# Rows of exponentials for graph attention: a trip through DRAM in place of transposes

## Chip, cores, metric

The kernel runs on one core of a Trainium2 chip. The metric is the device time of one execution in microseconds (us). Nearly all executions agree within 0.3%. Engines: TensorE does matmuls (PE in the profile; PEld are its weight loads), VectorE elementwise work (DVE), ScalarE activations and evictions (ACT), GpSimd (POOL) a little, SyncE issues DMAs (SP, its queue SPq).

## The reference, cut to what matters

64 graphs of 256 nodes with 256 features pass two layers: a graph attention layer (two attention steps, then a feed-forward) and a transformer-like layer with relations. Only the graph attention steps matter here, twice per graph:

```python
e = Wh1 + swapaxes(Wh2, 1, 2)          # [N, 1] + [1, N]
e = leaky_relu(e, 0.2)
att = softmax(where(adj > 0, e, NEG), axis=1)
h = matmul(att, Wh)
```

Because exp is monotonic, exp(leaky_relu(a + b)) is the larger of exp(a)exp(b) and exp(0.2a)exp(0.2b). So the kernel needs, on every partition, a row of exp(a) over all nodes and a row of exp(0.2a), and one number per partition for b.

## The kernel before

Graphs go in pairs; three pairs are in flight. A generator per pair yields after each step, and a small ordering rule hands the steps out: `yield us, later, stage` says how long the step takes on TensorE and how long to wait before the next step of the same pair is due. Steps of other pairs fill the wait. This only sets the order in which the program is written; the compiler's scheduler then orders each engine's queue. The argument below takes each engine to work through its queue in that order; experiment 5 shows ScalarE held so for 25.83 us by one operation.

```python
def addends(y, at, layer, pair, b):
    ...
    nc.scalar.activation(rise[:, 0], e1, AF.Exp, bias=shift[:, 0:1])
    nc.scalar.activation(rise[:, 1], e1, AF.Exp, bias=shift[:, 0:1], scale=ALPHA)
    nc.scalar.activation(ratio, e2, AF.Exp, scale=ALPHA - 1.0)
    return rise, ratio                       # rise: [128, 2, 2], four columns

def gat_weights(y, at, rise, ratio, adjT, empty, b):
    p = bank()
    for n in range(4):                       # L199: repeated column -> row on all partitions
        col = rise[:, n // 2, n % 2:n % 2 + 1]
        nc.tensor.transpose(p[:, n * P:(n + 1) * P], col.to_broadcast([P, P]), ident)
    up = work.tile([P, N], F32, name="up", bufs=2)
    nc.scalar.activation(up, p[:, :N], AF.Copy)
    ...                                      # e from p, ratio, up, adjT (VectorE)
    ...                                      # y scaled by 1/sums (ScalarE, L212)
```

A pair's graph attention is: product xT x w12 (L227), evictions, `addends`, `gat_weights`, product with e (L241), evictions, `addends`, `gat_weights`, product with e (L253), layer norm. Four transposes for each of 2 graphs and 2 layers make 16 per pair. The main filler is the feed-forward: L289 transposes x, ScalarE evicts yT (L290), L308 and L319 are its two matmul groups, L311 its activation.

## Time and profile before

| | before |
|---|---|
| time | 3452.26 us, median of 3 (3450.34 to 3454.68) |
| TensorE busy | 3344.4 us, 97% |
| VectorE, ScalarE busy | 55%, 40% |
| period (two pairs) | 213.4 us |
| first store of results | 225.7 us after the start |

A row of the profile's groups reads: line, engine, operation, tiles, shapes, count, then busy time in all, mean of one in ns, and idle time of the engine in front of it with what ended it. A row of waits reads: who waited for whom, us in total, times, longest. The lines themselves stand in the prediction.

### The profile page before, as it was taken

Reading aid. Unit: us, or ns where it says so; the run is one execution under the profiler, and the core shown is the slowest. Engines: PE = TensorE matmul, PEld = TensorE weight load, DVE = VectorE, ACT = ScalarE, POOL = GpSimd, SP = SyncE. Lnnn points to the kernel's source line nnn. Section 1 sums busy time; section 2 is a strip of 40 time slices with the busy share of each in tenths; the row PEclk is TensorE's granted clock in tenths of the full one; section 3 lists DMA queues with packets and bytes.
Section 4 is the critical chain, followed back from the end, with each engine's and each line's share of the span. In section 5 each row is a group of like instructions: output and inputs, shape, how many; then the busy total and the mean of one; then the engine's idle time right before and its main releaser. Section 6 shows DMA issues by size and latency. Waiting matters only on the chain.

```text
span 3449.2 us, 47284 instructions
## 1 busy us (share of the span) xinstructions
PE 3344.4 (97%) x18698; PEld 2150.5 (62%) x18698; DVE 1904.6 (55%) x4825; ACT 1371.0 (40%) x2586; POOL 481.5 (14%) x646
## 2 busy tenths in 40 slices
PE   7999999999999999999999999999999999999998
PEld 5566665666656566565665666656666566565655
DVE  5655645556456564555645555465554655546455
ACT  4343343433434334343444434444253442534332
POOL 0201111011110111111111111111111111111110
PEclk9999999999999999999999999999999999999999
DMA  5000010000100001000000100001000010000000
GB/s 166 7 25 19 13 37 7 25 19 13 37 7 25 25 7 37 7 28 23 20 25 7 41 10 25 19 7 43 7 25 19 7 43 7 25 19 1 13 1 14
DMA packets 66868, 78.22 MB, mean 23 GB/s; under 512 B 3280, under 2 KB 57680, under 8 KB 66640
## 3 DMA queue, kind: packets, MB, share of 16 engines
q1 hardware_dynamic: 66640, 75.13, 7.0%
q8 instruction: 150, 2.46, 0.3%
q14 instruction: 78, 0.64, 0.1%
HBM read 58.34 MB, written 16.78 MB: 22 GB/s over the span
## 4 chain that ended last, share of the span: by engine, by line
PE 87%; ACT 9%; DVE 2%; DMA 1%; issue 0%; SPq 0%; POOL 0%; POOLq 0%; DVEq 0%
PE ps L319 26%; PE ps L308 23%; PE ps L342 7%; PE ps L335 6%; PE ps L388 6%; PE ps L360 4%; PE ps L381 4%; PE ps L253 3%; PE ps L405 3%; ACT L189 2%; ACT yT L290 2%; PE ps L241 2%; PE ps L227 2%; PE ps L289 1%; ACT ff L311 1%; DVE e L206 1%
## 5 line engine op out<-in xcount | busy, mean ns | idle before, releaser
L276 POOL TENSOR_TENSOR rstd<-rstd,mhalf 128x2 f32<-128x2 f32 x256 | 206.1, 805 | 2729.3 <-DVE rstd L275 2713.4
L308 PE MATMUL ps<-yT,w_L_gnn_W 128*128 128x512 f32 x1024 | 482.7, 602 | 14.2 <-ACT yT L290 12.5
L308 PE MATMUL ps<-yT,w_L_gnn_w_ff 128*128 128x512 f32 x1024 | 482.5, 602 | 14.1 <-ACT yT L290 12.5
L319 PE MATMUL ps<-w_L_gnn_w_ff,ff 128*128 128x256 f32 x2048 | 450.2, 379 | 0.0
L319 PE MATMUL ps<-w_L_gnn_W,ff 128*128 128x256 f32 x2048 | 449.9, 379 | 0.0
L319 PEld LDWEIGHTS ps<-w_L_gnn_W,ff 128*128 128x128 f32 x2048 | 389.1, 190 | 66.6 <-issue 15.3
L319 PEld LDWEIGHTS ps<-w_L_gnn_w_ff,ff 128*128 128x128 f32 x2048 | 389.0, 190 | 66.0 <-issue 14.8
L374 DVE TENSOR_TENSOR m<-a,adjT 128x512 f32<-128x512 f32 x512 | 327.0, 688 | 175.6 <-ACT a L365 134.9
L266 DVE TENSOR_TENSOR x<-ps,x 128x512 f32<-128x512 f32 x256 | 176.1, 688 | 444.3 <-PE ps L319 330.7
L311 ACT ACTIVATE ff<-ps,c_L_gnn_b_ff 128x512 f32<-128x512 f32 x256 | 176.0, 687 | 448.2 <-PE ps L308 448.2
L365 ACT ACTIVATE a<-ps 128x512 f32<-128x512 f32 x512 | 264.4, 602 | 216.3 <-PE ps L360 216.1
L337 DVE TENSOR_TENSOR v<-ps,b_L_gnn_bv 128x512 f32<-128x512 f32 x128 | 88.1, 689 | 400.5 <-PE ps L335 400.5
L308 PEld LDWEIGHTS ps<-yT,w_L_gnn_W 128*128 128x128 f32 x1024 | 183.0, 190 | 199.2 <-issue 174.1
L308 PEld LDWEIGHTS ps<-yT,w_L_gnn_w_ff 128*128 128x128 f32 x1024 | 183.1, 190 | 198.9 <-issue 174.2
L290 ACT ACTIVATE yT<-ps 128x512 f32<-128x512 f32 x192 | 110.2, 592 | 479.8 <-PE ps L289 479.8
L311 ACT ACTIVATE ff<-ps,c_L_gnn_b 128x512 f32<-128x512 f32 x256 | 175.9, 687 | 292.8 <-PE ps L308 292.4
L335 PE MATMUL ps<-wv,yT 128*128 128x512 f32 x512 | 235.4, 592 | 0.0
L229 ACT ACTIVATE xw<-ps 128x260 f32<-128x260 f32 x128 | 45.7, 379 | 456.0 <-PE ps L227 456.0
L394 DVE RECIPROCAL s<-ps 128x256 f32<-128x256 f32 x128 | 224.0, 1750 | 0.0
L273 DVE BATCH_NORM_STATS2 st<-x 128x6 f32<-128x256 f32 x512 | 192.7, 418 | 8.6
L206 DVE SCALAR_TENSOR_TENSOR e<-ps,ratio,up 128x256 f32<-128x256 f32 x256 | 115.7, 475 | 141.2 <-ACT up L201 141.2
L335 PEld LDWEIGHTS ps<-wv,yT 128*128 128x128 f32 x512 | 97.3, 190 | 122.5 <-issue 122.2
(81 smaller groups left out, 4290.1 us busy)
## 6 DMA issues: line engine op xcount, KB each, us to landing
xT<-in_xT SPq DMA_DIRECT2D x32, 512.0 KB, 4.6
adjT<-in_adjT SPq DMA_DIRECT2D x32, 512.0 KB, 3.9
x<-in_x SPq DMA_DIRECT2D x32, 512.0 KB, 4.2
out<-x SPq DMA_DIRECT2D x32, 512.0 KB, 3.2
w_L_gnn_w_ff<-in_L_gnn_w_ff SPq DMA_DIRECT2D x2, 1024.0 KB, 11.3
w_L_gnn_W<-in_L_gnn_W SPq DMA_DIRECT2D x2, 1024.0 KB, 7.0
wv<-in_L_gnn_Wv SPq DMA_DIRECT2D x2, 256.0 KB, 7.1
w_L_gnn_W1T<-in_L_gnn_W1T SPq DMA_DIRECT2D x1, 256.0 KB, 6.1
```

The costliest lines, as they stand in the source:

```text
L273: nc.vector.bn_stats(st[:, j, :], r[:, 2 * b + j, :])
L276: nc.gpsimd.tensor_tensor(rstd, rstd, mhalf[:, :2], ALU.pow)
L290: nc.scalar.activation(yT[:, :, b * N:(b + 1) * N], pt.rearrange("p (c n) -> p c n", c=KC), AF.Copy)
L308: nc.tensor.matmul(p1, lhsT=w1[:, c, m * P:(m + 1) * P], rhs=yT[:, c, :], start=c == 0, stop=c == KC - 1)
L311: nc.scalar.activation(h, p1, func, bias=b1[:, m:m + 1])
L319: nc.tensor.matmul(p2[:, j * D:(j + 1) * D], lhsT=f[m][:, k * P:(k + 1) * P], rhs=w2[:, m, :], start=m == 0, stop=m == NF - 1)
L335: nc.tensor.matmul(ps, lhsT=yT[:, c, at:at + P], rhs=wv[:, c].rearrange("p r m -> p (r m)"), start=c == 0, stop=c == KC - 1)
L342: nc.tensor.matmul(ps, lhsT=w[:, d, c * P:(c + 1) * P], rhs=yT[:, d, :], start=d == 0, stop=d == KC - 1)
L365: nc.scalar.activation(a, ps[o], AF.Exp)
L374: nc.vector.tensor_tensor(m, a, adj, ALU.mult)
L388: nc.tensor.matmul(po[o * DH:(o + 1) * DH, :N], lhsT=v[:, jc, at:at + DH], rhs=ms[o][:, jc * N:(jc + 1) * N], start=r == 0 and jc == 0, st ...
L394: nc.vector.reciprocal(s, po[:, N:])
```

## The change

The row is fetched by DMA, so that TensorE gives up the transposes: `rise` is scattered to a row in DRAM, and that row is read back onto all 128 partitions. To hide the latency, the steps are ordered with longer delays; the load of the next pair and the store of the results move to later places.

```diff
+    scratch = ctx.enter_context(tc.tile_pool(name="scratch", bufs=4, space=bass.MemoryType.DRAM))
 ...
-    p = bank()
-    for n in range(4):
-        col = rise[:, n // 2, n % 2:n % 2 + 1]
-        nc.tensor.transpose(p[:, n * P:(n + 1) * P], col.to_broadcast([P, P]), ident)
-    up = work.tile([P, N], F32, name="up", bufs=2)
-    nc.scalar.activation(up, p[:, :N], AF.Copy)
+    row = scratch.tile([1, 4 * P], F32, name="row")
+    nc.sync.dma_start(row.rearrange("o (n p) -> p (o n)", p=P), rise.rearrange("p n j -> p (n j)"))
+    rows = work.tile([P, 2, N], F32, name="rows", bufs=4)
+    nc.sync.dma_start(rows.rearrange("p n i -> p (n i)"), row.to_broadcast([P, 4 * P]))
 ...
-            yield 1.75, b * 1.6, None            # after the first layer's product
+            yield 1.75, b * 6.5, None
 ...
-            yield 0.5, b * 3.4, None             # after each graph's weights
+        yield 0.0, 3.4, None
 ...                                              # the same in the second layer
-        nc.sync.dma_start(out[...], x)
-        yield 3.44, 0.0, None
+        yield 3.44, 5.0, None
+        nc.sync.dma_start(out[...], x)
```

In the new kernel the first product with e is L239, the second still L253.

More of the change, by code (lines that the diff above doesn't have):

```diff
@@ L191, in addends, with gat_weights @@
         nc.scalar.activation(ratio, e2, AF.Exp, scale=ALPHA - 1.0)
-        return rise, ratio
-    def gat_weights(y, at, rise, ratio, adjT, empty, b):
-        p = bank()
-        for n in range(4):
-            col = rise[:, n // 2, n % 2:n % 2 + 1]
-            nc.tensor.transpose(p[:, n * P:(n + 1) * P], col.to_broadcast([P, P]), ident)
-        up = work.tile([P, N], F32, name="up", bufs=2)
-        nc.scalar.activation(up, p[:, :N], AF.Copy)
+        row = scratch.tile([1, 4 * P], F32, name="row")
+        nc.sync.dma_start(row.rearrange("o (n p) -> p (o n)", p=P), rise.rearrange("p n j -> p (n j)"))
+        rows = work.tile([P, 2, N], F32, name="rows", bufs=4)
+        nc.sync.dma_start(rows.rearrange("p n i -> p (n i)"), row.to_broadcast([P, 4 * P]))
+        return rows, ratio
+    def gat_weights(y, at, rows, ratio, adjT, empty, b):
         e = work.tile([P, 2, N], F32, name="e", bufs=4)
@@ L205, in gat_weights @@
             k = 2 * b + j
-            nc.vector.scalar_tensor_tensor(e[:, j], p[:, N:], ratio[:, j:j + 1], up, op0=ALU.mult, op1=ALU.max)
+            nc.vector.scalar_tensor_tensor(e[:, j], rows[:, 1], ratio[:, j:j + 1], rows[:, 0], op0=ALU.mult, op1=ALU.max)
             nc.vector.scalar_tensor_tensor(e[:, j], adjT[:, k], empty[:, k:k + 1], e[:, j],
@@ L230, in gat_layers @@
             a.append(addends(y, D + 2, 0, pair, b))
-            yield 1.75, b * 1.6, None
-        if pair + 1 < NPAIR:
-            loaded[pair + 1] = load(pair + 1)
+            yield 1.75, b * 6.5, None
         for b in range(2):
             e.append(gat_weights(y, D + 2, *a.pop(0), adjT, empty, b))
-            yield 0.5, b * 3.4, None
+        yield 0.0, 3.4, None
         for b in range(2):
@@ L244, in gat_layers @@
             a.append(addends(z, D, 1, pair, b))
-            yield 1.75, 0.4 + b * 0.6, None
+            yield 1.75, b * 6.5, None
         for b in range(2):
             e.append(gat_weights(z, D, *a.pop(0), adjT, empty, b))
-            yield 0.5, b * 3.4, None
+        if pair + 1 < NPAIR:
+            loaded[pair + 1] = load(pair + 1)
+        yield 0.0, 3.4, None
         for b in range(2):
```

## The prediction

> **What bounds the kernel now.** I read the page first: busy shares, then the chain that ended last. The chain gives 87% of the span to TensorE, so the question is only what happens to TensorE's queue.
>
> ```profile
> span 3449.2 us, 47284 instructions
> PE 3344.4 (97%) x18698; PEld 2150.5 (62%) x18698; DVE 1904.6 (55%) x4825; ACT 1371.0 (40%) x2586; POOL 481.5 (14%) x646
> PE 87%; ACT 9%; DVE 2%; DMA 1%; issue 0%; SPq 0%; POOL 0%; POOLq 0%; DVEq 0%
> q1 hardware_dynamic: 66640, 75.13, 7.0%
> ```
>
> TensorE is idle for 3449 - 3344 = 105 us in all. VectorE and ScalarE have half their time to spare, the DMA engines nine tenths. The list of waits says where the 105 us lie; the start takes most of the rest.
>
> ```profile
> PE ps L199 <- ACT rise L189: 29.6, 46, 0.9
> PE ps L308 <- ACT yT L290: 25.0, 34, 0.7
> PE ps L253 <- ACT xw L212: 21.0, 16, 3.0
> ```
>
> L199 are the transposes to be removed; they also head the list of waits, because they follow two exps that follow an eviction. L253 is the second layer's product, L308 the feed-forward behind its own transposes (L289). To see what L199 really holds of the queue I read TensorE's timeline in the middle of the run (start, length, instructions, idle before). The pattern repeats every 213.4 us with two pairs of graphs in it.
>
> ```profile
> 1505.31 1.04 PE L289 MATMUL ps<-ident,x 128*128 128x128 f32 x8
> 1506.18 0.60 PE L199 MATMUL ps<-ident,rise 128*128 128x128 f32 x4
> 1507.31 0.65 PE L199 MATMUL ps<-ident,rise 128*128 128x128 f32 x4 [0.52 <-ACT rise L189]
> 1508.07 3.70 PE L308 MATMUL ps<-yT,w_L_gnn_W 128*128 128x512 f32 x8
> ...
> 1518.52 0.60 PE L199 MATMUL ps<-ident,rise 128*128 128x128 f32 x4
> 1520.04 0.65 PE L199 MATMUL ps<-ident,rise 128*128 128x128 f32 x4 [0.92 <-ACT rise L189]
> 1520.53 3.60 PE L308 MATMUL ps<-yT,w_L_gnn_W 128*128 128x512 f32 x8
> 1525.32 1.99 PE L253 MATMUL ps<-xw,e 128*128 128x256 f32 x8 [1.20 <-ACT xw L212]
> ...
> 1562.85 1.04 PE L199 MATMUL ps<-ident,rise 128*128 128x128 f32 x8
> 1563.72 3.60 PE L308 MATMUL ps<-yT,w_L_gnn_w_ff 128*128 128x512 f32 x8
> ...
> 1587.85 1.04 PE L289 MATMUL ps<-ident,x 128*128 128x128 f32 x8
> 1589.63 3.70 PE L308 MATMUL ps<-yT,w_L_gnn_w_ff 128*128 128x512 f32 x8 [0.74 <-ACT yT L290]
> ```
>
> Read from start to start, eight transposes with no wait take 1563.72 - 1562.85 = 0.87 us. A group with a wait takes 1508.07 - 1506.18 = 1.89 or 1520.53 - 1518.52 = 2.01. One period has groups of 1.88, 2.01, 1.88 and 0.87: 6.65 us.
>
> **What the Trainium skill says.** "DMA: Bandwidth & Descriptors", section "Anatomy of one DMA", puts a fixed cost near 2 us on a DMA, mostly the receipt of the last write, heaviest where the target is HBM. The trace fits: the 512 KB output store lands a median 3.2 us after issue (2.9 at best). The same page, "Two DMAs through the same engine are not ordered", says that a DMA reading what another wrote must wait for the first one's semaphore before it is issued: so two landings in series, which no DMA of this trace shows. Its "Rules for kernel authors" say that a non-contiguous last dimension becomes one descriptor per element: the first new DMA scatters 512 elements of 4 bytes. The nearest thing here, the 2 KB load of a1 in small runs, kept SyncE 0.65 us to issue against 0.37 for a 512 KB load. "TensorE: Matmul & The Clock Gate", "Part 4: PE-mode transpose", has some 275 ns for a transpose; the trace has 273 ns for one alone but 0.87/8 = 109 ns in a row, and I use the latter.
>
> **Removed.** Per layer and pair eight transposes on TensorE, two evictions of 387 ns on ScalarE (128 in all, 50 us of an engine with slack) and one PSUM bank per graph. VectorE's first operation of a weight reads SBUF in place of PSUM; it is 475 ns of an engine with slack, worth nothing by itself. Only TensorE's part counts. All 64 groups have 110 us from start to start. Three (4.2, 4.66, 1.56) lie in the start, where data were waited for; three of 0.87 follow; the 58 of the regular part hold 97 us. The wait of 1.2 us at L253, once a period, should go too, since more work is now placed before it: 15 x 1.2 = 18. Sum 97 + 18 + 3 = 118 us.
>
> **Given back between transposes and feed-forward.** Where L199 stood between L289 and L308 it covered the eviction of yT. Without it the step takes 1589.63 - 1587.85 = 1.78 us, not 0.87: 0.91 us more. Following the order in which the program hands its steps out, that was the case once per pair: 29 x 0.91 = 26 us. Left: 92 us, or a period of about 207.2.
>
> **Added.** Per graph and layer a scatter of 2 KB to DRAM and a read of 256 KB onto all partitions, 128 of each: 33.5 MB more written into SBUF beside 78, on engines 7% busy. No bandwidth bound. The matter is latency. From the end of the product to the exps takes 0.95 us (52.64 + 1.90 to 55.48 at the start). For the scatter I estimate 3.3 us to landing (the store's 3.2 minus its bulk, plus 32 tiny elements for each of 16 engines), for the broadcast 2.8, and from first weight operation to the next product 2.75 (46.34 to 49.08). Sum 9.8 us. The new delays of 6.5 and 3.4 in the order of the steps place, between a layer's product for the second graph and the next product for the first, six feed-forward steps of 1.72: 10.3 us, and 1.75 more for the first graph itself. So the chain fits with some 2 us to spare, provided SyncE isn't held up. It shares its one queue with the loads (512 KB each) and the store, which stands just before the first scatter: each in front costs perhaps 1.3 us. I allow 8 us in the whole run for waits of this kind.
>
> **The start is the loss I am surest of.** SyncE issues all weights in order.
>
> ```profile
> 28.11 0.38 SPq L92 DMA_DIRECT2D b_L_gnn_b<-in_L_gnn_b  x1
> 28.61 0.52 SPq L59 DMA_DIRECT2D xT<-in_xT  x1
> 31.87 5.41 PE L253 MATMUL ps<-xw,e 128*128 128x256 f32 x16 [3.04 <-ACT xw L212]
> ```
>
> Today the first pair's rows need no DMA, and its second layer's product starts at 31.87, having waited only for engines. After the change its first scatter cannot be issued before 28.6 and lands behind two 1 MB weights, issued at 26.0 and 27.4, that need 7.0 us: near 36.5. The broadcast lands at 39.5 to 45 (next pairs' loads may stand before it), the first layer's product starts at 43 to 48, and the second layer's another 10 to 11 us later, at 54 to 59. Nothing else is there to do for TensorE. Loss 22 to 27 us, less a little because the second pair's inputs, waited for today, are then there: 22.
>
> **Sum.** 3452 - 92 + 22 + 8 = 3390 us. I put the middle at 3386, because the gap between L289 and L308 may be partly filled by the next pair's first product, which now stands two steps later and needs nothing from ScalarE.
>
> **Rivals.**
> 1. *The DMA latency takes the place of the wait removed.* If scatter and broadcast need 9 us together in place of 6, or a load in front of them holds SyncE, TensorE waits at L241 and L253 (old lines) 1 us or more in each of 58 layers: 3440 and above. For it: two landings in series, small elements, one queue. SyncE also waits long for buffers today (1924 us before loads of adjT). Against it: feed-forward steps were deliberately placed to cover it, and the layers of graph attention don't fall together with the attention that frees those adjT buffers.
> 2. *Everything is covered and the start costs little*, as the order may let scatters pass loads: 3452 - 92 + 10 = 3370, or 3345 if the 26 us given back are also filled.
> 3. *The transposes were free anyway*, hidden under weight loads or other waits. Against it: start-to-start times show each group pushing L308 back by 0.87 to 2 us on an engine without slack. It would give 3452.
>
> **Range and chances.** Threshold for faster by 2% is 3383; my middle lies 3 us above it, so this is nearly a coin toss, pulled down by the waits of rival 1, which have a long tail, and up by rival 2. Slower by 2% (3521) would need more than 2 us lost in each of the 64 layers beyond the gain. Eight in ten: 3355 to 3425.
>
> **What would show it.** In the changed kernel: no transposes of rise; a period of about 207 us; TensorE's busy time down by some 75 us; L308's waits for yT risen from 25 to about 50 us; waits of the two graph products below 15 us after the start; TensorE's first feed-forward product near 67 us, not at 45.19. Scatter landing at 3 to 4 us and broadcast at 2.5 to 3.5. Wrong if the graph products wait over 1 us each time, if the scatter needs 5 us or more, or if the start moves by less than 10 us.

## The result, and the profile after

The changed kernel takes 3941.97 us (median of 4, 3932.68 to 3944.01) against 3453.47 us: ratio 1.1409, interval 1.1392 to 1.1426. It is 14% slower. Ratios here and below are the mean time of one kernel's fast runs over that of the other's of the same rounds, so they are not quite the ratio of the medians.

From the page of the changed kernel: busy shares, the chain that ended last by engine, and the two new DMAs (count, size, median us from issue to landing).

```profile
span 3941.8 us, 46427 instructions
PE 3436.4 (87%) x18186; PEld 2185.1 (55%) x18186; DVE 1944.9 (49%) x4825; ACT 1269.9 (32%) x2398; POOL 496.9 (13%) x646
PE 60%; DMA 23%; DVE 9%; ACT 5%; issue 2%; POOL 1%; SPq 0%; POOLq 0%; DVEq 0%
rows<-row SPq DMA_DIRECT2D x128, 256.0 KB, 4.5
row<-rise SPq DMA_DIRECT2D x128, 2.0 KB, 9.5
```

The 512 transposes are gone (18698 to 18186 matmuls), and DMA, 1% of the chain before, is 23% of it. The scatter of 2 KB takes twice as long to land as the broadcast of 256 KB. From the list of waits of TensorE and VectorE (who waited for whom, us in total, times, longest):

```profile
DVE e L206 <- DMA rows<-row: 851.1, 81, 16.7
PE ps L239 <- ACT xw L212: 248.7, 35, 28.0
PE ps L253 <- ACT xw L212: 138.8, 28, 16.2
PE ps L308 <- ACT yT L290: 56.2, 64, 9.8
```

TensorE waits for scaled y (L212), that for VectorE's weights e (L206), and that for the broadcast rows. One chain in the middle of the run, from the timeline of all engines (start, length, what, idle before):

```profile
1519.05 1.28 ACT L191 ACT_TABLE_LOAD   x1
...
1520.96 1.41 SPq L195 DMA_DIRECT2D row<-rise  x2
...
1531.12 0.81 SPq L197 DMA_DIRECT2D rows<-row  x2
1535.54 0.88 DVE L206 SCALAR_TENSOR_TENSOR e<-rows,ratio 128x256 f32<-128x256 f32 x2 [13.89 <-DMA rows<-row]
...
1538.31 6.47 PE L239 MATMUL ps<-xw,e 128*128 128x258 f32 x16 [7.65 <-ACT xw L212]
```

The scatter is issued at 1520.96 and the broadcast can go at 1531.1: 10.1 us. The broadcast takes 4.4, the weights 2.8. TensorE has run out of other steps at 1530.66 and waits 7.65 us. Then the product itself is slow: sixteen matmuls in 6.3 us from start to start, where they take 3.5 us otherwise (3.48 in an undisturbed group of d_long). The windows of the same stretch say why (bounds, length, busy time per engine, granted clock, DMA share, GB/s):

```profile
1538.30:1544.70 6.40, 6.39 (x17) 5.17 (x18) 0.92 (x6) 5.11 (x12) 0.00 (x0) 0.57 0.00 0
1544.70:1555.00 10.30, 10.30 (x49) 8.85 (x47) 0.16 (x1) 0.96 (x4) 0.00 (x0) 1.00 0.05 0
```

TensorE's granted clock is 0.57 behind the gap and 1.00 after it. In windows of half a microsecond it is 1.00 for the first 3 us of the gap, 0.50 from there until 5.3 us after the matmuls have begun again, and 1.00 from then on. So a long wait costs more than its length.

The books: TensorE is idle for 3942 - 3436 = 505 us, before for 105: +400. Its busy time should have fallen by the 76 us of the transposes to 3268 but is 3436: +168, which I put down to the slow clock (mean granted clock 0.939 against 0.999; with the same order of steps and no DMA, b_old_way below, the clock is 0.998 and busy time only 9 us above before). 400 + 168 - 76 = 492, which is the difference of the two spans. By place: the first store of results comes at 313.4 us in place of 225.7 (88 us lost at the start); from there to the store of the 29th pair, 14 periods, it takes 3381 us in place of 2988 (393), and what follows 247 in place of 236 (12). In the middle of the run the period is 239.6 in place of 213.4. One period has waits of 7.65, 6.28, 6.07 and 2.75 us at the four groups of products, 22.8 in all, and 8.7 us of slow matmuls behind them. Those 31.5 us are nearly the whole distance to the predicted period of 207.2.

### The profile page after: what moved, and what is told of

Its sections match the earlier page's. It is cut to its first block, busy times and chain, and to the rows that moved or that the text cites. A ratio compares the mean times of both kernels' runs of the same rounds, so it can differ in the third digit from the quotient of the medians.

```text
span 3941.8 us, 46427 instructions
## 1 busy us (share of the span) xinstructions
PE 3436.4 (87%) x18186; PEld 2185.1 (55%) x18186; DVE 1944.9 (49%) x4825; ACT 1269.9 (32%) x2398; POOL 496.9 (13%) x646
## 4 chain that ended last, share of the span: by engine, by line
PE 60%; DMA 23%; DVE 9%; ACT 5%; issue 2%; POOL 1%; SPq 0%; POOLq 0%; DVEq 0%
DMA row<-rise 15%; PE ps L319 14%; PE ps L308 12%; DMA rows<-row 7%; PE ps L342 6%; PE ps L335 5%; PE ps L388 5%; PE ps L360 3%; PE ps L253 3%; PE ps L381 3%; PE ps L239 3%; PE ps L405 2%; PE ps L227 2%; DVE e L206 2%; ACT yT L290 2%
## 5 line engine op out<-in xcount | busy, mean ns | idle before, releaser
L206 DVE SCALAR_TENSOR_TENSOR e<-rows,ratio 128x256 f32<-128x256 f32 x256 | 114.6, 478 | 856.0 <-DMA rows<-row 851.1
L308 PE MATMUL ps<-yT,w_L_gnn_w_ff 128*128 128x512 f32 x1024 | 486.6, 614 | 32.6 <-ACT yT L290 32.6
L308 PE MATMUL ps<-yT,w_L_gnn_W 128*128 128x512 f32 x1024 | 472.8, 602 | 23.6 <-ACT yT L290 23.6
L319 PE MATMUL ps<-w_L_gnn_W,ff 128*128 128x256 f32 x2048 | 460.7, 384 | 0.0
L319 PEld LDWEIGHTS ps<-w_L_gnn_W,ff 128*128 128x128 f32 x2048 | 397.0, 194 | 64.0 <-issue 8.1
L239 PE MATMUL ps<-xw,e 128*128 128x258 f32 x512 | 194.8, 559 | 254.8 <-ACT xw L212 248.7
L212 ACT ACTIVATE xw<-xw,rs 128x258 f32<-128x258 f32 (+1 forms) x256 | 116.4, 501 | 840.4 <-DVE rs L209 840.4
L290 ACT ACTIVATE yT<-ps 128x512 f32<-128x512 f32 x192 | 107.3, 593 | 685.9 <-PE ps L289 685.9
L308 PEld LDWEIGHTS ps<-yT,w_L_gnn_w_ff 128*128 128x128 f32 x1024 | 188.3, 194 | 242.3 <-issue 200.3
L239 PEld LDWEIGHTS ps<-xw,e 128*128 128x128 f32 x512 | 145.5, 293 | 317.0 <-ACT xw L212 283.3
L308 PEld LDWEIGHTS ps<-yT,w_L_gnn_W 128*128 128x128 f32 x1024 | 184.1, 190 | 234.9 <-issue 199.3
L253 PE MATMUL ps<-xw,e 128*128 128x256 f32 x512 | 162.2, 473 | 144.0 <-ACT xw L212 138.8
L266 DVE TENSOR_TENSOR x<-ps,x 128x512 f32<-128x512 f32 x256 | 175.3, 685 | 226.9 <-PE ps L319 159.9
```

Source lines behind the costliest of these rows:

```text
L206: nc.vector.scalar_tensor_tensor(e[:, j], rows[:, 1], ratio[:, j:j + 1], rows[:, 0], op0=ALU.mult, op1=ALU.max)
L239: nc.tensor.matmul(ps[:, :D + 2], lhsT=e[b][:, j, i * P:(i + 1) * P], rhs=y[:, 2 * b + j, :D + 2], start=j == 0, stop=j == 1)
L253: nc.tensor.matmul(ps[:, i * D:(i + 1) * D], lhsT=e[2 + b][:, j, i * P:(i + 1) * P], rhs=z[:, 2 * b + j, :D], start=j == 0, stop=j == 1)
L308: nc.tensor.matmul(p1, lhsT=w1[:, c, m * P:(m + 1) * P], rhs=yT[:, c, :], start=c == 0, stop=c == KC - 1)
L319: nc.tensor.matmul(p2[:, j * D:(j + 1) * D], lhsT=f[m][:, k * P:(k + 1) * P], rhs=w2[:, m, :], start=m == 0, stop=m == NF - 1)
```

## The experiments

What made the scatter take 10 us was the question. Its packets do not take that time. The DMA line of the changed kernel in the window from 1543 to 1558 us, in 40 slices of 0.375 us, shows the busy tenths of the engines:

```profile
DMA  0000006001400000000000000000000005399789
```

Two scatters, issued at 1544.4 and 1545.7, show up in three slices near 1545.3 and 1546.6; then nothing moves for over 8 us until the broadcast begins. The scatter's time is a wait for its completion. Three explanations fit so far: writes to neighbouring addresses hold each other up; the number of elements counts; or any small store to DRAM is confirmed late. A fourth, that the new order of steps costs the time, had to be excluded too.

**1. a_probe: six kinds of small store, in the kernel before** (the edit condensed).

```diff
+        if b == 1 and pair >= 3:      # in addends, nothing reads the target
+            near:    [1, 512]  in DRAM, 512 pieces of 4 B side by side, as in the change
+            far64:   512 pieces of 4 B, 64 B apart    far512: 512 B apart
+            joined:  [128, 4]  in DRAM, 128 pieces of 16 B    wide512: the same, 512 B apart
+            onchip:  512 pieces of 4 B, 8 B apart, into SBUF
```

> The kernel before with one dead store added per layer from the fourth pair on, of the same 2 KB of rise, whose landing is read from the trace; nothing waits for it, so the time should stay within 0.5% of 3452 us. Six targets in turn. Theory 1 (adjacent 4-byte writes to DRAM are finished one after the other): 'near' (512 elements of 4 bytes side by side, as in the change) 9 to 10 us, 'far64' and 'far512' (512 elements of 4 bytes, 64 or 512 bytes apart) 3 to 5 us, 'joined' (128 pieces of 16 bytes) 3 to 6 us, 'onchip' (512 elements of 4 bytes into SBUF) about 3 us. Rival 2 (the number of elements counts, wherever they go): near, far64, far512 and onchip all 9 to 10, joined and wide512 (128 pieces of 16 bytes, 512 bytes apart) 3 to 4.5. Rival 3 (any small store to DRAM is confirmed late): all 9 to 10 except onchip.

Measured: 3454.68 us (2 runs, ratio 1.0004). From the DMA issues of this kernel (the two "far" cases are merged by name there and left out):

```profile
near<-rise SPq DMA_DIRECT2D x10, 2.0 KB, 10.9
joined<-rise SPq DMA_DIRECT2D x10, 2.0 KB, 2.1
wide<-rise SPq DMA_DIRECT2D x9, 2.0 KB, 3.9
onchip<-rise SPq DMA_DIRECT2D x9, 2.0 KB, 2.0
```

By line, far64 landed in a median of 4.5 us and far512 in 1.8. The lines of far512:

```profile
L207 SPq DMA_DIRECT2D far<-rise x10: 359/360/367, 286.0 to 3232.0; - x10
DMA to landing us min/median/max: 1.7/1.8/2.0
```

Near, far64 and wide512 stood in the first layer, where loads of 512 KB are about, the others in the second, so 2 us of differences between them are not to be read. The main result stands clear of that: 512 elements of 4 bytes land in under 2 us when they are 512 bytes apart and in 10.9 when side by side. The number of elements is not it, and small stores to DRAM are not late as such. Theory 1 is left.

**2. e_probe2: the pitch alone, all in the second layer.**

```diff
+        d = scratch.tile([4 * P, w], F32)      # w = 1, 2, 4, 8, 16: pitch 4 to 64 B
+        nc.sync.dma_start(d[:, 0:1].rearrange("(n p) o -> p (n o)", p=P), src)
+        # "quarter": one column of rise alone, 128 elements at a pitch of 4 B
```

> The kernel before with one dead store per pair (second layer, where no load is about), read for its landing alone: 512 elements of 4 bytes at a pitch of 4, 8, 16, 32 and 64 bytes (pitcha to pitche), and 'quarter', 128 elements of 4 bytes at a pitch of 4. Theory 1 (writes that fall into the same small block of DRAM are finished one after the other): landing falls with the pitch in step with the elements per block, about 9.5, 5 to 6, 3 to 4, 2 to 3, 2 us, and quarter stays near pitcha (8 to 10 us), as its blocks are as full. A rival that counts adjacent elements in all: quarter at a quarter of pitcha's excess, some 3.5 to 4 us.

3455.43 us. Landing:

```profile
pitchd<-rise SPq DMA_DIRECT2D x5, 2.0 KB, 2.2
pitche<-rise SPq DMA_DIRECT2D x5, 2.0 KB, 1.9
quarter<-rise SPq DMA_DIRECT2D x5, 0.5 KB, 7.3
pitcha<-rise SPq DMA_DIRECT2D x5, 2.0 KB, 8.7
pitchb<-rise SPq DMA_DIRECT2D x5, 2.0 KB, 3.3
pitchc<-rise SPq DMA_DIRECT2D x4, 2.0 KB, 2.7
```

At pitches of 4, 8, 16, 32 and 64 bytes the store lands in 8.7, 3.3, 2.7, 2.2 and 1.9 us. A quarter of the elements at pitch 4 still takes 7.3. So how densely they lie decides, hardly how many there are. The step from 4 to 8 bytes is far steeper than the halving that I had expected; what happens inside the memory to make it so, these runs do not show. The Trainium skill, "DMA: Bandwidth & Descriptors", section "Specifications", says that below 512 B the DMA engine does a read-modify-write. That would fit with neighbours waiting for one another, but it is argued, not shown; and the page does not separate lone small writes, which land in 1.9 us here, from crowded ones.

**3. b_old_way: the new order of steps with the old transposes.**

```diff
 # against the changed kernel
-        row = scratch.tile(...)    # both DMAs
+        p = bank(); 4 transposes; up = copy        # as before
```

> The changed kernel's order of steps, delays and moved load and store, but the rows by 16 transposes per pair as before: no new DMA. Theory (the DMA chain costs it): 3430 to 3480 us, period about 213 us. Rival 4 (the new order of steps itself, or the moved load and store, costs it): over 3700 us.

3473.03 us, ratio 1.0057 (1.0040 to 1.0074). Period 214.2, first store at 239.7. The order of steps and the moved load and store cost 19 us by themselves, no more: rival 4 falls. One of its waits matters for the prediction:

```profile
PE ps L308 <- ACT yT L290: 47.2, 64, 0.7
```

With all transposes still there, this wait is nearly doubled against the 25.0 of the kernel before: in the new order the transposes stand elsewhere, not between L289 and L308.

**4. c_rows16: the same two DMAs, but with four values side by side.**

```diff
-        nc.sync.dma_start(row.rearrange("o (n p) -> p (o n)", p=P), rise...)
+        nc.sync.dma_start(row.rearrange("o (p n) -> p (o n)", p=P), rise...)
-        rows = work.tile([P, 2, N], F32, name="rows", bufs=4)
+        rows = work.tile([P, P, 4], F32, name="rows", bufs=4)
 ...      # VectorE reads rows[:, :, n] with a stride of 16 bytes
```

> The change with one edit: the row in DRAM is laid out so that each partition's four values lie together, 128 pieces of 16 bytes in place of 512 of 4; VectorE then reads rows with a stride of 16 bytes. Theories 1 and 2: the scatter lands in 3 to 5 us in place of 9.5, the wait at the first product (L239) falls from some 7 us to 1 to 3, time 3520 to 3650 us. Rival 3: landing and time as in the change, 3900 or more. If the strided read slows VectorE, its first operation on e rises above 478 ns.

3485.37 us, ratio 1.0095 (1.0078 to 1.0112): 457 of the 488 us are back, more than expected. From its DMA issues, its waits and its groups:

```profile
row<-rise SPq DMA_DIRECT2D x128, 2.0 KB, 2.6
```

```profile
PE ps L240 <- DVE e L207: 81.0, 29, 23.0
```

```profile
L207 DVE SCALAR_TENSOR_TENSOR e<-rows,ratio 128x256 f32<-128x256 f32 x256 | 164.9, 675 | 388.5 <-DMA rows<-row 388.4
```

The scatter lands in 2.6 us, and TensorE's wait at the first product (now L240) falls from 249 to 81 us, of which 23 lie in the start. The strided read costs VectorE 675 ns in place of 478, on an engine with time to spare. The layout also helped what is issued beside the scatters: the 512 KB loads of xT landed in 9.1 us in the median in the change (one issued between two scatters in 8.9) and in 4.6 here. The kernel is still 1% slower than before: its period is 213.8 and its first store comes at 255.1. In one period, the first layer's product waited 2.73 and 1.30 us. The windows behind the two waits:

```profile
1555.90:1561.10 5.20, 5.20 (x16) 4.20 (x17) 1.08 (x6) 5.06 (x12) 0.00 (x0) 0.67 0.00 0
1597.30:1601.30 4.00, 3.81 (x16) 2.95 (x17) 1.70 (x7) 3.25 (x9) 0.00 (x0) 1.00 0.00 0
```

The clock was 0.67 for 5.2 us behind the first and 1.00 behind the second. That the length of the wait alone decides is not shown: p_all below has a wait of 2.91 us with the clock at 1.00 behind it. The chain in front of the 2.73 us reads 3.4 us from the product's end to the scatter's issue, 4.4 to its landing, 3.8 for the broadcast and 3.3 for the weights, 14.9 in all, while TensorE ran dry after 12.2.

**5. d_long: the scatter left as it is, with delays of 15 us in place of 6.5.**

```diff
-            yield 1.75, b * 6.5, None      # both layers
+            yield 1.75, b * 15.0, None
```

> The change with its two delays of 6.5 us after the products raised to 15, so that more independent steps are queued between the DMAs and their use; the DMAs stay as they are. If the chain's length against the queued work is all that matters: waits of L239 and L253 after the start nearly gone, granted clock back to 0.99 there, period 207 to 215 us, time 3500 to 3580 with the loss at the start left. Rival (the DMAs get later in step with the queue, or there is not enough other work): over 3750 us.

4145.08 us, ratio 1.1999: a clear miss, 200 us slower than the change itself. The products do not wait any more, but others do. From the timeline:

```profile
2198.77 1.04 PE L289 MATMUL ps<-ident,x 128*128 128x128 f32 x8
...
2215.44 0.91 ACT L212 ACTIVATE xw<-xw,rs 128x258 f32<-128x258 f32 x2 [25.83 <-DVE rs L209]
...
2217.36 1.06 ACT L290 ACTIVATE yT<-ps 128x512 f32<-128x512 f32 x2
...
2218.48 4.07 PE L308 MATMUL ps<-yT,w_L_gnn_w_ff 128*128 128x512 f32 x5 [18.67 <-ACT yT L290]
```

The feed-forward's transposes were done at 2199.8. Their eviction (L290) stood in ScalarE's queue behind the scaling L212, which waited 25.83 us for VectorE, which waited for the rows. TensorE's product had been moved back; ScalarE's and VectorE's operations of the same chain had not been moved far enough behind, and those engines work in order. In all L308 waited 308 us for yT, against 25 in the kernel before and 56 in the change.

**6. i_long16: the delays of 15 us, with rows of 16 bytes.**

> The delays of 15 us of d_long, with rows of 16 bytes in place of elements of 4. If d_long was slow because VectorE and ScalarE, each in order, stood at operations waiting for late rows while TensorE's other work waited for them: rows are now there in time, and the time falls to 3440 to 3530 us, with no wait above 5 us on TensorE after the start. If long delays are bad by their order of steps alone: over 3800.

3613.64 us, ratio 1.0463. The late rows were worth 531 of d_long's excess, as the theory says, but the time lies above the range that I expected, a miss: L308 still waits 126 us for yT, 7.0 at most. So 15 us are too much on their own account as well. How the rest splits, I did not follow up.

**7. f_tr3: rows of 16 bytes, transposes in the first three pairs.**

```diff
+        if pair < 3:
+            return rise, ratio          # and the four transposes in gat_weights
```

> Rows of 16 bytes as in c_rows16, but the first three pairs get their rows by transposes, so that the start waits for no DMA. If the start's loss is the scatter and broadcast of the first pairs: the first store of results moves from 255 us (c_rows16) back to 226 to 240, time 3455 to 3475; the period stays at 213.8. If the loss has another cause: no change, 3485.

3471.12 us, ratio 1.0054. The first store comes at 237.4 in place of 255.1. The first pairs' DMAs are most of what the start of c_rows16 lost; the rest is that of b_old_way (239.7), so it belongs to the order of steps.

**8. k_act and 9. l_act_tr3: the scatter issued by ScalarE.**

```diff
-        nc.sync.dma_start(row.rearrange("o (p n) -> p (o n)", p=P), ...)
+        nc.scalar.dma_start(row.rearrange("o (p n) -> p (o n)", p=P), ...)
```

> Rows of 16 bytes, and the scatter issued by ScalarE behind its exps in place of SyncE, where the loads of x and xT stand in front of it. If those loads are what stretches the first layer's chain: scatter of the first layer lands in 2 to 3.5 us in place of 4.4 and is issued 1 us earlier, wait at the first layer's product from 2.7 and 1.3 us to below 1, period 207.5 to 210.5 us, time 3395 to 3440. Rival (issue on ScalarE costs as much, or the broadcast is now behind the loads): 3470 to 3500.

> The two edits together: transposes for the first three pairs, scatter from ScalarE. If both gains add: 3370 to 3415 us, faster than the kernel before by 1 to 2.4%. If the period doesn't fall: 3455 or more.

3487.10 us (ratio 1.0100) and 3469.08 us (1.0049): no gain over c_rows16 and f_tr3, so both hoped-for gains were missed. In the first layer the scatter landed in 3.7 to 4.7 us, as from SyncE (4.0 to 4.3), against 1.4 in the best of the second layer. The place in SyncE's queue is not what stretches it. That the loads of x and xT, which are under way at that time, do so is likely but not shown.

**10. n_tr3_d10: f_tr3 with a delay of 10 in the first layer only.**

```diff
-            yield 1.75, b * 6.5, None      # first layer
+            yield 1.75, b * 10.0, None
```

> f_tr3 (rows of 16 bytes, transposes in the first three pairs) with the first layer's delay 10 in place of 6.5: two more feed-forward steps before its product. If the wait of 2.7 and 1.3 us at that product, with the slow clock after it, is all that separates the period of 213.8 from the predicted 207.2: period 207 to 209.5, time 3380 to 3410. Rival (the wait moves to ScalarE's or VectorE's queue, as in d_long): 3450 to 3500.

3396.65 us (3395.25 to 3397.27), ratio 0.9834 (0.9818 to 0.9851): 1.7% faster than the kernel before, and the best of all. Its period is 209.3. From its page and its waits:

```profile
PE 3297.3 (97%) x18234; PEld 2101.6 (62%) x18234; DVE 1987.8 (59%) x4825; ACT 1270.9 (37%) x2410; POOL 496.6 (15%) x646
```

```profile
PE ps L269 <- DVE e L222: 6.7, 15, 0.8
PE ps L255 <- ACT xw L228: 2.6, 1, 2.6
```

TensorE's busy time is 47 us below the kernel before's, and the products of graph attention (now L255 and L269) hardly wait. A new wait has come up instead, 20.4 us in all of the second feed-forward group for its activation. The old transposes with a delay of 10 were not run, so how much of the gain over the kernel before is the missing transposes and how much the order of steps is not separated.

**11. p_all and 12. r_all_d10: the store back in its old place, the first three pairs in the old order.**

```diff
-        yield 3.44, 5.0, None
         nc.sync.dma_start(out[...], x)
+        yield 3.44, 0.0, None
 # first three pairs: delays and place of the load as before
 # r_all_d10: also 10.0 in the first layer
```

> f_tr3 with the store of results back where it was and the first three pairs in the order of steps of before: the loads of x then come behind the first layer's scatters in SyncE's queue. Start back to about 226 us for the first store (f_tr3: 237.4). If the loads stretch the first layer's scatter, its wait falls by 1 to 2 us too: 3390 to 3440 us; if only the start gains, 3455 to 3462.

> p_all and the delay of 10 in the first layer together. If both terms are real and add: 3365 to 3400 us, faster than the kernel before by 1.5 to 2.6%. If the delay moves the wait elsewhere: slower than p_all.

3496.86 us (ratio 1.0128) and 3403.79 us (0.9859). The start gained (first store at 229.4 and 226.9), but p_all is slower than either forecast for it, with a period of 216.2: its first product waits 1.46 and 0.94 us for one pair and 2.91 and 0.92 for the other, and L308 waits 1.72 in place of 0.74. With the store moved back, the transposes of the feed-forward, which hold TensorE for 0.87 us, fall between the two products, and 20 feed-forward matmuls stand before the second in place of 24. That the ordering rule allows more for these transposes than they take is the likely reason; it was not tested.

```profile
1588.35 2.01 PE L260 MATMUL ps<-xw,e 128*128 128x258 f32 x8 [2.91 <-ACT xw L228]
```

Behind this wait the granted clock stayed at 1.00. With 10 us the same kernel reaches a period of 210.4 and falls just short of what I expected of it.

## Why the prediction was wrong

**The bound, and what the transposes hold: right as far as the runs go.** TensorE is the bound. n_tr3_d10, without the transposes in all but three pairs, has 47 us less of TensorE's busy time and a period of 209.3, 2.1 us above the 207.2 worked out; the kernel before has 213.4. Its order of steps differs too, so the worth of the transposes alone is not measured.

**What is given back at L308: the number right, the reason not.** Its waits for yT rose from 25 to 50 us in c_rows16, as foreseen, and to 56 in the change. But b_old_way, with all transposes kept, has 47.2: the new order of steps exposes the eviction of yT, not the removal of the transposes.

**"For the scatter I estimate 3.3 us to landing (the store's 3.2 minus its bulk, plus 32 tiny elements for each of 16 engines)": this is the step that failed.** The chain that was to fit with some 2 us to spare left waits of 2.75 to 7.65 us at the products. The mechanism, a chain of latencies set against queued work, was right; this term of the sum was mis-sized. It measured 9.5 us in the median and 10.1 in the chain shown. I took the latency of a large store and added something per element; but it is not a cost per element. It is the neighbourhood of the elements in DRAM, and nothing in the profile of before held such a store. The nearest thing was a load of 2 KB, of which I used only the issue time; its landing, 6.3 us in the crowded start, stood in the trace too, but a load into SBUF is not this store. With one edit to where the elements lie (c_rows16), 457 of the 488 us were gone.

**Two smaller terms of the same sum were too low.** The exps: 0.95 us was read at the start of the run, where no table load stands in front of them. In the middle ScalarE first loads a table, 1.28 us, and from the product's end to the scatter's issue it is some 2.5 us. Those loads were in the profile of before, too. The broadcast: 2.8 estimated, 4.5 measured. The last leg, 2.75, was right (2.77). So the chain was some 20 us, not 9.8, against the 12 us of queued work that I had counted correctly (10.3 + 1.75; TensorE ran dry 12.2 us after the first graph's product). These terms count by themselves: in c_rows16 the scatter lands in 2.6 us in the median, less than the 3.3 assumed, and the time, 3485 us, still lies above the range of 3355 to 3425. Its chain of 14.9 us has 3.4, 3.8 and 3.3 us in the three other terms, and its first-layer scatter needs 4.4.

**A term was missing: the slow clock behind a gap.** The Trainium skill, "TensorE: Matmul & The Clock Gate", section "What's actually happening", says that the array runs at half its clock after at least one idle window of some 3.4 us. I knew of waits of 1 us and more as a rival and priced them at their length. The trace agrees for the gap of 7.65 us, where the clock fell to 0.50 some 3 us into the gap; shorter gaps are in the list below. I put 168 us of busy time down to it.

**The loss at the start: 22 us foreseen, 88 measured, 29 with a fast scatter.** TensorE's first feed-forward product came at 83.4 us, not near 67; with the fast scatter at 70.7. The reason given (SyncE's queue, and two landings in series in each of two layers before the first feed-forward) holds for the larger part, and it was again the scatter that was mis-sized. But 14 of the 29 us are lost in b_old_way too, which has no new DMA: they belong to the order of steps. Transposes in the first three pairs bring back 18 of the 29.

**Rival 1 was the right one, and I gave it too little.** I had it end at 3440 "and above", from scatter and broadcast needing 9 us together; their medians were 9.5 and 4.5, some 14. The range assumed that the scatter would be off by fractions; since it had, like the broadcast's 2.8, no measurement behind it, the range should have been worked out with two or three times its estimate in the sum.

**What I then believed of delays was also wrong** (d_long): that more work queued before the product is enough. A delay of 10 in one layer helped, 15 in both did harm.

## What to carry to other kernels

Before putting a DMA round trip in the place of engine work, measure the landing of exactly that DMA in an idle corner of the old kernel: here a dead store (10.9 us) told in one run what the large store (3.2 us) could not. If, as here, single 4-byte values must go to DRAM, do not lay values of different partitions side by side; let each partition write its 16 bytes in one piece and take the stride on the reading side. When a latency is to be hidden by ordering, look at the queue of every engine of the chain, not only TensorE's: d_long suggests moving all of the chain's operations behind the filler, which no run here tested. Count a long gap on TensorE at more than its length: 22.8 us of waits in one period here had 8.7 us of slow matmuls behind them.

## What the Trainium skill lacked or had wrong

- "DMA: Bandwidth & Descriptors" warns of descriptors for single elements and of writes below 512 B, but does not say that neighbouring small writes to DRAM delay the landing: 512 elements of 4 bytes land in 8.7 us at a pitch of 4 B, 3.3 at 8 B and 1.9 at 64 B, and 128 of them still take 7.3 at a pitch of 4 B. The same 512 elements into SBUF, 8 B apart, land in 2.0 us.
- The same page, in a section headed for DMAs issued by GpSimd, puts the fixed cost of a DMA near 2 us; the prediction used it for SyncE's. Small stores from SyncE in the quiet second layer agree (1.8 to 2.2 us); the 256 KB broadcast of a 2 KB row took 4.5 us in the median in the change and 3.8 in c_rows16, and no page gives a figure for such a read.
- "TensorE: Matmul & The Clock Gate" names about 3.4 us of idleness as what slows the array. Here a gap of 2.73 us (c_rows16) was followed by a mean granted clock of 0.67 over 5.2 us: in half-microsecond windows it stayed at 1.00 through the gap and the first 1.3 us of matmuls, and then was 0.50 for about 3.4 us. Gaps of 2.91 us (p_all) and 1.30 us (c_rows16) left it at 1.00. So shorter gaps than the page names can cost, but not every one does; what decides between them is not shown.
